# A product and its use placed in different steps, a last layer-1 group of four cut into two, one and one, and a bias as three bf16 terms

## The chip, the cores and the metric

The kernel runs on one core of a Trainium2 chip. The metric is the device time of one execution in microseconds. Three runs of the kernel before gave 1993.61, 1996.18 and 1997.73 us; the median is 1996.18.

The engines are named as in the profile: PE is TensorE (PEld its weight loads), DVE is VectorE, ACT is ScalarE, POOL is GpSimd, and SP is the engine whose queue issues most of the DMAs.

## The reference

Four graph layers run one after the other over 128 graphs of 64 nodes with 128 features. Each adds its result to its input and normalises. Weights, `_layernorm` and `einsum` letters are as usual; everything is float32.

```python
def ssp(x): return softplus(x) - log(2)
# layer 0: d = adj; a filter from 20 Gaussians of d, cut off at 5
f = exp(coeff * (d[..., None] - offsets) ** 2)
W = (ssp(f @ fw1 + fb1) @ fw2 + fb2) * rcut(d)[..., None]
x = layernorm(x + ssp(einsum('bjf,bijf->bif', x @ w_in2f, W) @ ow1 + ob1) @ ow2 + ob2)
# layer 1: the same form with 64 Gaussians and adj as the weight, twice
x = layernorm(x + ...)
# layer 2: three graph convolutions, nA = D^-1/2 (adj + 1) D^-1/2
h = elu(elu(x @ W0 + b0))
h = elu(nA @ (h @ W1) + b1)
x = layernorm(x + nA @ (h @ W2) + b2)
# layer 3: one more, with a small epsilon in the degree
x = layernorm(x + relu((nA3 @ x) @ W3.T + b3))
```

## The kernel before

Two graphs make a *pair* (128 nodes, one per partition), so there are 64 pairs. Only edges that exist are computed: a compaction on DVE (`MAX8`, `FIND_INDEX8`, `MATCH_REPLACE8`, lines 913 to 976) sorts each node's edges into a fixed number of slots. It runs for the first part beside the edge work of the first pairs.

The main loop (line 1504) has 386 iterations. Pairs 0 to 63 are layer 0, 64 to 127 are layer 1, and each pair's edge slots are cut into three chunks, one per iteration. One chunk passes through four stages in three iterations: `filter_in` (PE product `px` on L1410, then two ACT operations that make `h`), `gather` (PE product `pg` on L1436 from a one-hot matrix `hot`, copied by ACT to `g`), `filter_out` (PE product `pw` on L1423) and `message` (DVE `m` on L1451, from `pw` and `g`). After the third chunk eight DVE reductions (L1467, the `sums` queue) add messages into `agg`. PSUM is full: `px` and `pg` have one buffer of two banks each, `pw` has two banks, and a pool `sps_n` with two banks (tag `n`, function `bank`) serves every other product.

When four pairs (a *group*, `GS = 4`) have their sums, the node work of the group follows: `node_after` (products `u`, `o`, `back`, with `na`, `nh`, `no`, `ny` as their uses on ACT and DVE, and a layer norm). In layer 0, `zero_share` (`zT`, `zs`) comes first. After layer 1, `graph_convs` computes layers 2 and 3 of the group: products `gx`, `gh`, `hw`, `nT`, `o`, `sup`, and their uses `gxt`, `em`, `er`, `gy`, `nTs`, `gz`. `node_before` (`xT`, `y`) prepares the features of the group that comes next.

These functions are Python generators. Each `yield` ends a *step*; the loop takes one step from a queue at certain places of an iteration, so that their instructions stand between those of the edges. There are the queues `nodes` (`node_before` and `node_after`) and `convs[0]` and `convs[1]` (graph convolutions of even and odd groups). A step of the kernel before usually holds a product *and* its use:

```python
        y = tiled(f"gy_{name}_{k}")
        nc.vector.tensor_copy(y, ps)      # straight after the four matmuls into ps
```

At the end `in_order` ties every engine's instructions to the order in which the program wrote them, so an engine never takes a later instruction first. Behind the loop a `while` takes steps from the queues in turn until all are empty.

The layer norm takes `bn_stats` and `bn_aggr` per pair on DVE, a power (`rs`, L1175) and one normalisation per pair (L1178) on POOL.

Of the kernel before, what the change touches and what calls it, by code (L numbers as in the profile page):

```python
# [18 lines left out]
P = 128  # L19
A = 64  # L20
# [557 lines left out]
def sparse_stack(ctx: ExitStack, tc: tile.TileContext, t: dict, out: bass.AP, flag):  # L578
# [16 lines left out]
    NG = NP // GS  # L595
# [5 lines left out]
    cpt = ctx.enter_context(tc.tile_pool(name="scompact", bufs=1))  # L601
# [112 lines left out]

    def dram_ap(ap, offset, dims):
        return bass.AP(tensor=ap.tensor, offset=ap.offset + offset, ap=dims)
# [4 lines left out]
    fence, last, kind = None, None, None  # L721

    def act(out_, in_, func, **kw):
        nonlocal fence, last, kind
        now = func == AF.Sin
        if kind is None or now != kind:
            fence = last
            if not now:
                ctx_ = tc.issue_after(fence.ins) if fence is not None else nullcontext()
                with ctx_:  # L730
                    fence = nc.scalar.preload_act_table_set("natural_log_exp_and_others")
            kind = now
        with tc.issue_after(fence.ins) if fence is not None else nullcontext():
            last = nc.scalar.activation(out_, in_, func, **kw)  # L734
        return last
# [24 lines left out]
    ones = const.tile([1, P], F32, name="ones")  # L760
# [76 lines left out]
    def load_row(name, times=1):  # L837
        b = const.tile([1, times * C], F32, name=f"r_{name}")
        nc.scalar.dma_start(b, dram_ap(t[name], 0, [[0, 1], [0, times], [1, C]]))
        return b  # L840
# [206 lines left out]
    def run(queue, n):  # L1047

        while queue and n:
            try:  # L1050
                next(queue[0])
                n -= 1
            except StopIteration:
                queue.popleft()

# [61 lines left out]
    g["b3"] = load_row("L3_gnn_b", GS)  # L1117
# [16 lines left out]
    def late_constants():  # L1134
# [21 lines left out]
        for i in (2, 3):  # L1156
            g[f"blk{i}"] = const.tile([P, GS, P], F32, name=f"blk{i}")
            nc.gpsimd.memset(g[f"blk{i}"], 0.0)
            yield


    def bank(name):
        ps = ps_n.tile([P, 512], F32, tag="n", name=name)
        return ps, ps.rearrange("p (s c) -> p s c", s=GS)

    def layernorm(y, dst, n, name):

        stats = node.tile([P, n, 6], F32, tag=f"st{n}", name=f"st_{name}")
        mv = node.tile([P, n, 2], F32, tag=f"mv{n}", name=f"mv_{name}")
# [3 lines left out]
        rstd = node.tile([P, n], F32, tag=f"rs{n}", name=f"rs_{name}")  # L1173
        nc.vector.tensor_scalar(rstd, mv[:, :, 1], LN_EPS, None, ALU.add)  # L1174
        nc.gpsimd.tensor_tensor(rstd, rstd, neg_half[:, 0:n], ALU.pow)  # L1175
        yield
# [9 lines left out]
    def node_before(layer, q):  # L1186
# [3 lines left out]
        flat, ps = bank(f"xT_{name}")  # L1190
        for s in range(GS):
            nc.tensor.transpose(ps[:, s, :], x_all[:, q * GS + s, :], ident)
        xt = node.tile([P, 512], F32, tag="xt", name=f"xt_{name}")
        nc.vector.tensor_copy(xt, flat)
        yield
        flat, ps = bank(f"y_{name}")
        for s in range(GS):
# [3 lines left out]
        y = node.tile([P, GS, C], F32, tag="y", name=f"ys_{name}", bufs=3)  # L1201
        act(y, ps, AF.Copy)
        feats[layer, q] = y

        xs = x_all[:, q * GS : (q + 1) * GS, :]
        nc.gpsimd.tensor_tensor(xs, xs, w["c2"].unsqueeze(1).to_broadcast([P, GS, C]), ALU.add)
# [5 lines left out]
    def zero_share(q, agg):  # L1212

        rows = node.tile([P, GS, A], F32, tag="zr", name=f"zr_{q}")
        for s in range(GS):
            nc.sync.dma_start(rows[:, s, :], perm[q * GS + s][:, 0:A])
# [5 lines left out]
        flat, ps = bank(f"zT_{q}")  # L1222
        for s in range(GS):
            nc.tensor.transpose(ps[:, s, :], zblk[:, s, :], ident)
        zt = node.tile([P, GS, P], F32, tag="zt", name=f"zt_{q}", bufs=1)
        act(zt, ps, AF.Copy)
        yield
        flat, ps = bank(f"zs_{q}")
        y = feats[0, q]
        for s in range(GS):  # L1230
            nc.tensor.matmul(ps[:, s, :], lhsT=y[:, s, :], rhs=zt[:, s, :], start=True, stop=True)
        nc.vector.scalar_tensor_tensor(agg, ps, zero_filter, agg, ALU.mult, ALU.add)
        yield

    def node_after(layer, q, agg):
# [4 lines left out]
        codes = node.tile([P, GS * P], BF16, tag="cb", name=f"cb_{name}")  # L1240
        nc.sync.dma_start(codes, dram_ap(code_dram[layer], q * GS * P, [[0, P], [1, GS * P]]))
        if layer == 0:
            yield from zero_share(q, agg)
        u, _ = bank(f"u_{name}")
# [3 lines left out]
        a = node.tile([P, 512], F32, tag="na", name=f"na_{name}", bufs=1)  # L1248
        act(a, u, AF.Abs, bias=w["c1"])
        h = node.tile([P, 512], F32, tag="nh", name=f"nh_{name}", bufs=1)  # L1250
        nc.vector.tensor_scalar(h, u, w["c1"], 0.0, ALU.add, ALU.max)
        yield
        act(a, a, AF.Exp, scale=-1.0)

        back = node.tile([P, GS, P], F32, tag="bk", name=f"bk_{name}", bufs=1)
        nc.vector.tensor_scalar(
            back.rearrange("p s i -> p (s i)"), codes, row[:, 0:1], None, ALU.is_equal
        )
        act(a, a, AF.Ln, scale=0.5, bias=half)
# [3 lines left out]
        _, ps = bank(f"o_{name}")  # L1263
        for s in range(GS):
# [3 lines left out]
        o = node.tile([P, GS, C], F32, tag="no", name=f"no_{name}", bufs=1)  # L1268
        act(o, ps, AF.Copy)
        yield  # L1270
        _, ps = bank(f"back_{name}")
        for s in range(GS):
            nc.tensor.matmul(ps[:, s, :], lhsT=back[:, s, :], rhs=o[:, s, :], start=True, stop=True)  # L1273
        y = node.tile([P, GS, C], F32, tag="ny", name=f"ny_{name}", bufs=1)
        xs = x_all[:, q * GS : (q + 1) * GS, :]
        nc.vector.tensor_add(y, ps, xs)
        yield
        yield from layernorm(y, xs, GS, name)
        if layer == 1:
            convs[q % 2].append(graph_convs(q))  # L1280

    def elu(ps, bias, name, twice=False):

        m, r = big(f"em_{name}", 512), big(f"er_{name}", 512)
# [4 lines left out]
        if twice:  # L1289
# [4 lines left out]
        return r  # L1294

    def graph_convs(k):

        pairs = slice(k * GS, (k + 1) * GS)
        xs = x_all[:, pairs, :]

        def tiled(name):
            return big(name, GS * P).rearrange("p (s c) -> p s c", s=GS)

        def scaled(i):

            dinv, blk = g[f"dinv{i}"], g[f"blk{i}"]
            for h in range(2):
# [3 lines left out]
                    dinv[at, pairs].unsqueeze(2).to_broadcast([A, GS, A]), ALU.mult,  # L1311
                )

        def normal(i):

            _, ps = bank(f"nT{i}_{k}")
            for s in range(GS):
                nc.tensor.transpose(ps[:, s, :], g[f"blk{i}"][:, s, :], ident)
            nT = tiled(f"nTs{i}_{k}")
            dinv = g[f"dinv{i}"]  # L1320
            nc.vector.tensor_mul(nT, ps, dinv[:, pairs].unsqueeze(2).to_broadcast([P, GS, P]))
            return nT

        def times(name, lhs, rhs):

            _, ps = bank(f"{name}_{k}")
            for s in range(GS):
                nc.tensor.matmul(ps[:, s, :], lhsT=lhs(s), rhs=rhs(s), start=True, stop=True)  # L1328
            y = tiled(f"gy_{name}_{k}")
            nc.vector.tensor_copy(y, ps)  # L1330
            return y

        scaled(2)
        yield
        nT = normal(2)
        yield
        flat, ps = bank(f"gx_{k}")
        for s in range(GS):
            nc.tensor.transpose(ps[:, s, :], xs[:, s, :], ident)
        xt = big(f"gxt_{k}", 512)  # L1340
        nc.vector.tensor_copy(xt, flat)
        nc.gpsimd.tensor_tensor(xs, xs, g["b2"].unsqueeze(1).to_broadcast([P, GS, C]), ALU.add)
        yield
        flat, _ = bank(f"gh0_{k}")
        nc.tensor.matmul(flat, lhsT=g["W0"], rhs=xt, start=True, stop=True)
# [241 lines left out]
```

## Time and profile before

| | |
|---|---|
| median of three runs | 1996.18 us |
| profiled execution, its own time | 1989.18 us |
| its span, first to last instruction | 1987.4 us |
| granted PE clock over the span | 0.939 |
| busy: PE, DVE, ACT, POOL | 84%, 79%, 72%, 31% |
| HBM traffic | 107 GB/s |
| last chain by engine: PE, DVE, issue, ACT, POOL | 47%, 28%, 9%, 7%, 5% |

The span is the time between the first and the last instruction; the execution's own time has 1.8 us more around it. A busy share is an average over stages that have different limits. A wait row names the waiting instruction, the one that released it, the sum of the waits in us, how many there were, and the longest.

### The profile page before, as it was taken

To read this page: it belongs to the slowest core of one execution; us is meant where nothing else is said; L and a number is where in the kernel's file an instruction comes from. 1 tells how busy PE (TensorE), PEld (TensorE's weight loads), DVE (VectorE), ACT (ScalarE), POOL (GpSimd) and SP (SyncE) were. 2 spreads that over 40 slices of the span, in tenths; PEclk is the share of its full clock that TensorE was granted. 3 is DMA by queue.
4 is the path that set the end of the run, shared out by engine and by line. 5 is a ranking of instruction groups with operands and counts; after the bars stand their busy time and mean duration, and the time that the engine had idled before them with its cause. 6 is when DMAs were issued, how large, how long until landed. Compare 5 with 4: busy or idle time off the path is not lost.

```text
span 1987.4 us, 23539 instructions
## 1 busy us (share of the span) xinstructions
PE 1666.1 (84%) x6796; PEld 806.3 (41%) x6796; DVE 1578.6 (79%) x4249; ACT 1436.7 (72%) x1663; POOL 624.8 (31%) x899
## 2 busy tenths in 40 slices
PE   0298887888788999879989999999999999999874
PEld 0133333343333444334444444444444444444443
DVE  6588878988888777867767888888888887988863
ACT  1277767777677888758888788787787878787720
POOL 2423434432333222251111223233232232323243
PEclk9998888998888999989999999999999999999985
DMA  4354534443444444434656455445454445455300
GB/s 122 83 141 113 129 94 113 112 114 89 113 99 99 116 112 116 105 73 104 142 132 135 103 125 126 109 114 132 111 126 116 114 118 128 115 117 124 72 6 13
DMA packets 120256, 214.95 MB, mean 108 GB/s; under 512 B 41504, under 2 KB 68276, under 8 KB 120116
## 3 DMA queue, kind: packets, MB, share of 16 engines
q1 hardware_dynamic: 111456, 207.19, 44.1%
q0 software_dynamic: 4352, 5.02, 0.8%
q10 hardware_dynamic: 4308, 1.13, 0.3%
q8 instruction: 56, 0.92, 0.2%
q14 instruction: 84, 0.69, 0.1%
HBM read 200.92 MB, written 12.34 MB: 107 GB/s over the span
## 4 chain that ended last, share of the span: by engine, by line
PE 47%; DVE 28%; issue 9%; ACT 7%; POOL 5%; DMA 4%; SPq 0%; DVEq 0%; ACTq 0%; POOLq 0%
PE pw L1423 17%; PE pg L1436 10%; PE px L1410 8%; DVE agg L1467 7%; DVE m L1451 5%; ACT h L734 3%; DVE hot L1395 2%; DVE st L1171 2%; DVE mv L1172 2%; PE back L1273 2%; POOL x_all L1178 1%; PE y L1198 1%; ACT d L734 1%; PE o L1265 1%; PE hw L1328 1%
## 5 line engine op out<-in xcount | busy, mean ns | idle before, releaser
L734 ACT ACTIVATE g<-pg 128x752 f32<-128x752 f32 (+1 forms) x384 | 321.1, 836 | 295.3 <-PE pg L1436 270.1
L1467 DVE TENSOR_REDUCE agg<-m 128x16 f32<-128x336 f32 (+11 forms) x1024 | 417.7, 461 | 1.5
L1423 PE MATMUL pw<-h,w_L_gnn_fw 128*128 128x376 f32 x768 | 321.3, 545 | 107.9 <-DVE m L1451 104.6
L1175 POOL TENSOR_TENSOR rs<-rs,neg_half 128x4 f32<-128x4 f32 x64 | 98.3, 1536 | 951.7 <-DVE rs L1174 860.2
L1423 PE MATMUL pw<-h,w_L_gnn_W2T 128*128 128x432 f32 x768 | 335.4, 561 | 67.1 <-DVE m L1451 67.1
L1436 PE MATMUL pg<-hot,ys 64*128 64x376 f32 (+1 forms) x1536 | 383.9, 578 | 3.2 <-ACT g L734 3.2
L734 ACT ACTIVATE h<-h,half 128x752 f32<-128x752 f32 (+2 forms) x385 | 372.3, 967 | 12.5
L1451 DVE SCALAR_TENSOR_TENSOR m<-pw,c_L_gnn_b,g 128x432 f32<-128x432 f32 x384 | 240.3, 660 | 12.1 <-PE pw L1423 7.7
L1451 DVE SCALAR_TENSOR_TENSOR m<-pw,c_L_gnn_fb,g 128x376 f32<-128x376 f32 x384 | 216.4, 601 | 40.9 <-PE pw L1423 30.0
L1423 PEld LDWEIGHTS pw<-h,w_L_gnn_fw 128*128 128x128 f32 x768 | 143.6, 206 | 229.2 <-DVE m L1451 159.9
L1423 PEld LDWEIGHTS pw<-h,w_L_gnn_W2T 128*128 128x128 f32 x768 | 134.6, 194 | 223.4 <-DVE m L1451 131.1
L734 ACT ACTIVATE h<-px,c_L_gnn_b 128x864 f32<-128x864 f32 x192 | 187.2, 975 | 49.4 <-PE px L1410 49.4
L1436 PEld LDWEIGHTS pg<-hot,ys 64*128 64x128 f32 x1536 | 122.3, 195 | 211.4 <-ACT h L734 104.8
L1395 DVE SCALAR_TENSOR_TENSOR hot<-j,row,w 128x1128 f32<-128x1128 bf16 (+1 forms) x128 | 194.3, 1518 | 0.7
L1410 PE MATMUL px<-d,fw 32*128 32x376 f32 x768 | 178.8, 542 | 2.4 <-ACT d L734 2.4
L1410 PE MATMUL px<-d,w1t 64*128 64x432 f32 x768 | 178.7, 542 | 0.0
L734 ACT ACTIVATE h<-px,c_L_gnn_fb 128x752 f32<-128x752 f32 x192 | 169.4, 882 | 12.1 <-PE px L1410 3.3
L734 ACT ACTIVATE d<-d,neg_off 96x752 f32<-96x752 f32 (+1 forms) x128 | 145.2, 1134 | 0.0
L853 POOL DMA_INDIRECT rows<-comb,goes x64 | 65.2, 1018 | 130.5 <-DMA rows<-comb,goes 98.0
L1410 PEld LDWEIGHTS px<-d,fw 32*128 32x128 f32 x768 | 59.2, 188 | 113.9 <-issue 66.7
L1178 POOL TENSOR_SCALAR x_all<-ny,mv,rs 128x128 f32<-128x128 f32 x128 | 102.9, 813 | 3.3
L1410 PEld LDWEIGHTS px<-d,w1t 64*128 64x128 f32 x768 | 69.0, 187 | 56.8 <-issue 41.8
(208 smaller groups left out, 2029.5 us busy)
## 6 DMA issues: line engine op xcount, KB each, us to landing
d<-d_dram SPq DMA_DIRECT2D x128, 324.0 KB
w<-w_dram SPq DMA_DIRECT2D x128, 324.0 KB
w<-w_dram SPq DMA_DIRECT2D x128, 282.0 KB
j<-j_dram SPq DMA_DIRECT2D x128, 162.0 KB
j<-j_dram SPq DMA_DIRECT2D x128, 141.0 KB
d<-d_dram SPq DMA_DIRECT2D x192, 94.0 KB
x_all<-in_x_dram SPq DMA_DIRECT2D x8, 512.0 KB
cb<-code_dram SPq DMA_DIRECT2D x32, 128.0 KB
```

Of the source, the lines that this page charges most:

```text
L734: last = nc.scalar.activation(out_, in_, func, **kw)
L853: nc.gpsimd.indirect_dma_start(out=into, out_offset=bass.IndirectOffsetOnAxis(ap=at, axis=0), in_=rows, in_offset=None,)
L1171: nc.vector.bn_stats(stats[:, s, :], y[:, s, :])
L1172: nc.vector.bn_aggr(mv[:, s, :], stats[:, s, :])
L1175: nc.gpsimd.tensor_tensor(rstd, rstd, neg_half[:, 0:n], ALU.pow)
L1178: nc.gpsimd.tensor_scalar(dst[:, s, :], y[:, s, :], mv[:, s, 0:1], rstd[:, s : s + 1], ALU.subtract, ALU.mult,)
L1395: nc.vector.scalar_tensor_tensor(hots[n][:, 0:size], j[:, 0:size], near, wt[:, 0:size], ALU.is_equal, ALU.mult)
L1410: nc.tensor.matmul(ps[:, b, 0:n], lhsT=w["w1"][rows, :], rhs=d[rows, col : col + n], start=True, stop=True,)
L1423: nc.tensor.matmul(ps[:, 0 : c["size"]], lhsT=c["w"]["w2"], rhs=c["h"][:, b, :], start=True, stop=True)
L1436: nc.tensor.matmul(ps[:, b, 0:n], lhsT=y[rows, :], rhs=hots[c["n"]][rows, at], start=True, stop=True,)
L1451: nc.vector.scalar_tensor_tensor(messages[n][:, b, at], c["pw"][b][:, 0:size], c["w"]["b2"], c["g"][:, b, :], ALU.add, ALU.mult,)
L1467: nc.vector.tensor_reduce(av[:, :, :, r], v[:, :, :, BASES[layer][r] : BASES[layer][r] + CAPS[layer][r]], AX.X, ALU.add,)
```

## The change

- A step that ends in a PE product now yields `True`, and its use on DVE or ACT stands in the next step. A function `slot` takes one step of a queue; if it ended in a product, that queue is *owing*, and the next `slot` of a queue that is not empty first takes its own step and then the owed one.
- `node_before` has a queue of its own (`befores`). The order inside an iteration changes: sums, compaction, side work and the one-hot come first; then `filter_in`, the slots of nodes and befores; then `filter_out`, `message`, the first convs slot, Gaussians, `gather`, and the second convs slot (a second nodes slot when there are no convs).
- `GROUPS`: layer 1 has fifteen groups of four, then one of two pairs and two of one. Those three do not enter `nodes` and `convs`; each has a lane in `last`, gets two slots in an iteration, and goes from `node_after` straight into `graph_convs`.
- The pool of the compaction is closed at iteration 195, and a pool `srings` takes its place: four buffers per lane for the convs, and a block matrix `blocks` per lane in place of `blk2` and `blk3`.
- The last bias, a float32 row added by a float32 product with `ones` (L1368), is split once into three bf16 terms whose sum is the row; the product then has three rows in bf16.
- In the layer norm the power moves from the step of the statistics to the step of the normalisations; in `node_before` the addition of `c2` moves ahead of the product `y`; in `graph_convs` the normalised matrix for layer 2 is made after `hw1` instead of at the start, and the scaling for layer 3 right after `o2`. `zero_share` waits one step more after its loads.

The core of the diff:

```diff
+    GROUPS = [[slice(GS * q, GS * (q + 1)) for q in range(NP // GS)]] * 2
+    GROUPS[1] = GROUPS[1][:-1] + [slice(NP - 4, NP - 2), slice(NP - 2, NP - 1), slice(NP - 1, NP)]
...
+    def load_terms(name):
+        b = const.tile([1, C], F32, name=f"r_{name}")
+        nc.scalar.dma_start(b, t[name].rearrange("(o p) -> o p", o=1))
+        part_ = const.tile([1, 3, C], BF16, name=f"p_{name}")
+        for i in range(3):
+            nc.vector.tensor_copy(part_[:, i, :], b)
+            if i < 2:
+                nc.vector.tensor_sub(b, b, part_[:, i, :])
+        terms = const.tile([3, GS, C], BF16, name=f"t_{name}")
+        for s in range(GS):
+            nc.scalar.dma_start(terms[:, s, :], part_[0:1].rearrange("o i c -> o (i c)"))
+        return terms
...
         rstd = ...
         nc.vector.tensor_scalar(rstd, mv[:, :, 1], LN_EPS, None, ALU.add)
+        yield
         nc.gpsimd.tensor_tensor(rstd, rstd, neg_half[:, 0:n], ALU.pow)
-        yield
...
         nc.tensor.matmul(
             u, lhsT=w["o1"], rhs=agg.rearrange("f s r -> f (s r)"), start=True, stop=True
         )
+        yield True
         a = once("na", n, q)
         act(a, u, AF.Abs, bias=w["c1"])
+        act(a, a, AF.Exp, scale=-1.0)
         h = once("nh", n, q)
         nc.vector.tensor_scalar(h, u, w["c1"], 0.0, ALU.add, ALU.max)
         yield
-        act(a, a, AF.Exp, scale=-1.0)
...
         if layer == 1:
-            convs[q % 2].append(graph_convs(q))
+            if n < GS:
+                yield from graph_convs(q)
+            else:
+                convs[q % 2].append(graph_convs(q))
...
+    def slot(queue):
+        nonlocal owing
+        if not queue:
+            return
+        before, owing = owing, None
+        held = run(queue, 1)
+        if before is not None and before is not queue:
+            run(before, 1)
+        if held:
+            owing = queue
...
     for i in range(3 * N + 2):
+        run(sums, 3)
+        run(early, 7)
+        run(side, 1)
...
-            filter_in(c)
-        run(nodes, 1)
-        if c is not None and k == 0:
-            one_hot(n)
-        run(sums, 3)
-        run(early, 7)
-        run(side, 1)
+                one_hot(n)
+            filter_in(c)
+        slot(nodes)
+        if k < 2:
+            slot(befores)
+        for queue in last:
+            slot(queue)
         if c2 is not None:
             filter_out(c2)
             message(c2)
+        slot(convs[0])
         if k < 2 and n + 1 < N:
             gaussians(n + 1, k)
-        run(convs[0] or nodes, k == 2 or bool(convs[0]))
         if c1 is not None:
             gather(c1)
-        run(convs[1], 1)
+        slot(convs[1] if convs[0] or convs[1] else nodes)
+        for queue in last:
+            slot(queue)
```

## The prediction

> **What bounds the kernel now.** I read the page's busy shares first, then the busy time by stage, then the waits inside each stage, and last the end of the chain. The shares alone do not name a bound:
>
> ```profile
> span 1987.4 us, 23539 instructions
> ...
> PE 1666.1 (84%) x6796; PEld 806.3 (41%) x6796; DVE 1578.6 (79%) x4249; ACT 1436.7 (72%) x1663; POOL 624.8 (31%) x899
> ```
>
> The stages do. Columns: window, its length, then busy us (instructions) of PE, weight loads, DVE, ACT and POOL, then clock, DMA share, GB/s. The windows are layer 0 while edges are still compacted, the rest of layer 0, layer 1, and the tail after the last edge product.
>
> ```profile
> 100.00:620.00 520.00, 431.44 (x1636) 193.66 (x1635) 443.64 (x1687) 378.45 (x462) 185.11 (x340) 0.90 0.45 110
> 620.00:1030.00 410.00, 364.72 (x1512) 168.69 (x1510) 309.09 (x659) 334.70 (x408) 111.79 (x142) 0.95 0.46 112
> 1030.00:1900.00 870.00, 805.55 (x3422) 400.45 (x3421) 724.17 (x1519) 697.76 (x763) 259.07 (x290) 0.98 0.50 115
> 1904.00:1988.00 84.00, 44.53 (x166) 31.78 (x164) 38.93 (x109) 6.60 (x10) 35.20 (x43) 0.63 0.04 11
> ```
>
> In layer 1 PE is busy 93% and idle 64 us. In the first window it is idle 89 us, in the second 45. The waits of layer 1 say for what (us in total, times, longest):
>
> ```profile
> PE pw L1423 <- DVE m L1451: 63.9, 39, 3.2
> DVE nh L1251 <- ACT na L734: 51.4, 15, 4.6
> ...
> DVE ny L1276 <- PE back L1273: 15.6, 15, 2.1
> DVE gz L1374 <- PE o L1370: 12.7, 7, 1.9
> ...
> DVE em L1285 <- PE gh L1351: 8.3, 7, 1.3
> ```
>
> All of PE's idle time in layer 1 is the edge product `pw` waiting for the message `m` that frees its bank, and `m` is late because DVE stood still ahead of it, waiting for a node or conv product issued just before. DVE's waits of this kind (the rows shown, and `em` on L1345, `gz` L1359, `gy`, `xt`, `gxt`, `nTs`) add to 126 us; with 724 busy that is 850 of 870, so DVE and PE bound together. In the first window the same sum is nh 18.1 + zblk 11.2 + ny 8.6 + agg 4.8 + xt 0.3 = 43 us beside 444 busy of 520; PE waits 67.5 for `m`. In the second it is nh 21.7 + ny 17.5 + agg 14.1 + zblk 3.7 = 57 us; PE waits 40.4, of which one wait of 12.1 belongs to the `dinv` power on POOL, which stays.
>
> The tail lasts from the last `pw` (ends 1904.6) to 1987.4: 83 us in which no engine is busy 55%. It is one chain of four-pair operations, at a low clock: the `hw` product of four pairs takes 1.05 us at 1330 and 2.04 at 1957.7.
>
> **What the Trainium skill says.** "PSUM — Partial Sum Buffer", section Engine vs sequencer instructions: the queues of ScalarE, VectorE and GpSimdE are strict FIFO. The trace agrees: DVE idles up to 4.6 us at `nh` with ready messages behind it. The same page, section PSUM bank collisions raise a hardware error, says two engines must not read one bank at once; that is why `nh` waits for ACT's `na` although both read only `u` (at 1330 `na` ends at 1330.42 and `nh` starts at 1330.45). So this wait is not removed by a later place, only overtaken. "TensorE: Matmul & The Clock Gate", section Back-to-back issue gap, gives 518 cycles at 2.4 GHz for N=512 in bf16, 0.22 us; no bf16 product is in this trace.
>
> **The change part by part.** The sum is made against the profiled execution, 1989.18 us (the span and 1.8 around it); it lies 7.0 under the median 1996.18, and I carry the difference over to the median.
>
> *Steps that part product and use.* No steady instruction goes away. In the changed order of instructions the use of a product from the first slot stands behind the two messages (2 x 0.62 us) instead of ahead of sums and messages, and that of the convs' first slot behind the gather (0.83 us of PE). Of `nh`'s 3.0 us per wait, 1.2 is overtaken by the messages alone and more by the three reductions now ahead. What can be won is the smaller of DVE's product waits and PE's waits for `m`: 43 in the first window, 40.4 - 12.1 = 28 in the second, 64 in the third; together **135**. I take half, **-68**, for two reasons: ACT is busy 80% in layer 1 and `px` and `pg` have one buffer each, so it becomes late next; and 30 of 334 DVE uses now stand behind three reductions and a one-hot (1.2 + 1.5 us), holding their bank that long. Ends: 0 and -135; below nothing is the rival with the banks.
>
> *Order inside the iteration.* Sums, compaction, side work and one-hot move ahead of the node step on DVE; messages keep the same work before them. On SP the six or seven loads of a pair come behind the compaction's stores (some 0.6 us each); the first of them is used three iterations (14 us) later, which hides it; without that cover 8 parts x 2 layers x 3 stores x 0.6 = +29. The extra empty step between the `zr` loads and `zblk` costs nothing, since the nodes queue has two slots per iteration there; it may save some of the 11.2 us above. On POOL `pow` moves one step back to its normalisations and the `c2` addition one forward; POOL is busy 30% there: 0, at most +3.
>
> *Bias.* L1368 has 32 passes at some 0.5 us from start to start, 16 us; 18 bf16 products at the page's 0.22 are 4. PE is the bound of only part of layer 1, so of 12 I take **-6**; ends 0 and -12. The terms add five DVE operations on one partition (each under 0.3 us by the 128x64 rows) and four small loads on ACT's queue at the start; DVE stands idle from 39.6 to 53.6 for the `ad` landing and ACT until 79.8, so at most **+1**.
>
> *Pools and lanes.* Per-lane blocks replace two shared ones: five memsets on an idle POOL, 0 to +2. Closing the compaction pool makes the first memset wait for stores that ended long before.
>
> *The tail.* Groups of four end at pair 59; then come two, one and one, with two more `cb` loads and two more stores on SP, each as early as its lane. Before, group 14's convs and all of group 15 are left when the edges end. After, the order leaves the end of 13's convs, nearly all of 14's, and the lanes of two, one and one, taken in turn. From that order, with a 128x512 DVE operation at 0.69 us and a 128x128 one at about 0.25 (estimated from 0.69 less 384 elements at the same rate), DVE has 37 us left. POOL has 13 powers x 1.03, 28 normalisations x 0.78, and blocks and bias additions of some 7: 42 us. So POOL is the floor. The last pair's own chain is short: 11 products at 0.5, 15 DVE operations at 0.35, three layer norms at 0.65 on DVE and 1.8 on POOL, 7 ACT at 0.3 and 35 handovers at 0.05: some 22 us, with the store 25. Five lanes through in-order queues do not reach the floor; between 45 and 72 I take 58: **-25**.
>
> Sum: -68 - 6 - 25 + 1 = **-98**: own time 1891, on the level of the median **1898**.
>
> **The rivals.** (a) *ACT takes the bound.* For: ACT is busy 3.76 us per iteration in edges alone and DVE 4.2 of 5.0, so three engines are within 15% of each other. Against: ACT waits 116 us for `pg` in layer 1, so it has room. Steady gain a fifth, 14, with tail 22: 1960. (b) *All of it comes.* The clock of 0.90 in the first window rises too, since PE idles less; 135 + 12 + 30: 1819. (c) *The banks decide, and it is slower.* The pool `sps_n` has two banks for four queues. Before, the use was issued straight behind its product; now two products are open at once, and the third waits for a use issued only one slot earlier. Price: 30 uses behind the one-hot x 2.7 = 81, and the other 350 products at 0.3 each (messages and use, 1.24 + 0.69, less gather and `px` of 1.66 that PE does meanwhile) = 105; 186 against the 98: +88, 2084. It decides once a product waits on average over 98/382 = 0.26 us. Against it: PE has 2.6 us of own work between a conv product and the third one. (d) *The parts do not separate in layer 0,* where only the nodes queue has work: then the gain is layer 1's half and the tail, 32 + 6 + 25: 1933. The order of instructions speaks against it: `nh` stands behind the messages there too.
>
> **How the numbers follow.** Forecast 0.52; (a) 0.17; (b) 0.13; (d) 0.06; (c) 0.10; no change 0.02. A measurement of this kernel tells about 0.2%, 4 us, from nothing. Faster: all but (c) and no change, less a little of (a): 0.87; same 0.03; slower 0.10. The range leaves out (c) and most of (b): 1838 to 1964. The likeliest is 1898.
>
> **What would show it.** Right: in layer 1 `pw <- m` below 40 us, `nh <- na` below 20, `ny`, `gz`, `em`, `gy` nearly gone from DVE's waits, an iteration of 4.7 us instead of 5.0 (132 `h<-px` between 1230 and 1890); in the first window 4.5 instead of 4.8 (108 in 520); 55 to 60 us after the last `pw`, POOL busiest. Wrong: node and conv products (`o`, `hw`, `gh`, `nT`) waiting on PE for DVE or ACT uses, which is (c); ACT over 90% with `px <- h`, which is (a); a tail over 70 us.

## The result: slower by 1.5%

The changed kernel takes 2025.4 us (median of four runs, 2021.7 to 2027.3) where the kernel before takes 1995.0 in the same session: a ratio of 1.0148, 95% interval 1.0129 to 1.0168. Forecast were 1898 us and a range of 1838 to 1964. The profiled execution took 2027.3, its span 2025.5.

The busy shares of the changed kernel's page say as little as those of before: PE 83%, DVE 78%, ACT 71%, POOL 31%.

To compare stages, I cut both executions at the same work, not at the same time: at the start of `hot` of pairs 8, 52, 72, 120 and 124 (pairs 0 to 63 are layer 0). The busy time in such windows of the changed kernel (columns as in the prediction; pairs 8 to 52, 52 to 72, 72 to 120, and 124 to the end):

```profile
208.20:857.40 649.20, 539.17 (x2046) 245.95 (x2042) 506.03 (x1666) 457.09 (x568) 208.29 (x383) 0.90 0.40 101
857.40:1137.30 279.90, 236.21 (x917) 106.04 (x918) 198.09 (x408) 209.29 (x247) 63.40 (x55) 0.93 0.45 106
1137.30:1837.80 700.50, 646.93 (x2833) 325.50 (x2830) 597.48 (x1262) 572.16 (x627) 218.76 (x246) 1.00 0.51 121
1897.70:2025.50 127.80, 95.06 (x404) 56.60 (x402) 93.75 (x251) 54.64 (x74) 55.34 (x77) 0.83 0.14 35
```

The kernel before needs 610.6, 262.3, 710.8 and 146.5 us for the same; its first and third windows are

```profile
198.40:809.00 610.60, 521.55 (x2048) 237.85 (x2046) 502.89 (x1671) 461.59 (x568) 209.88 (x384) 0.91 0.45 108
...
1071.30:1782.10 710.80, 660.60 (x2832) 330.19 (x2831) 595.96 (x1251) 570.63 (x625) 215.65 (x242) 0.98 0.51 119
```

So layer 0 lost 39 + 18 us (and 7 more in pairs 0 to 8), layer 1 gained 10, and the end gained 19. The waits of pairs 8 to 52 show what layer 0 lost:

```profile
ACT h L740 <- PE px L1457: 107.6, 47, 8.5
...
DVE zblk L1254 <- DMA zr<-perm: 40.4, 11, 6.1
...
PE zT L1258 <- DVE zblk L1254: 38.0, 11, 6.6
...
PE o L1302 <- DVE nh L1298: 22.9, 11, 2.6
PE y L1232 <- DVE xt L1226: 21.8, 11, 3.5
...
PE pw L1470 <- DVE m L1498: 9.7, 13, 1.5
```

In the kernel before, the same stretch had

```profile
PE pw L1423 <- DVE m L1451: 70.0, 41, 4.6
...
DVE zblk L1220 <- DMA zr<-perm: 13.0, 6, 5.1
```

The wait that I wanted gone is gone: `pw` behind `m` was 70.0 us and is 9.7. In its place PE stands eleven times, once in each group, at `zT`, at `o` and at `y`; `px`, queued behind them, comes late, and ACT waits 107.6 us for it. `y` waits for `xt`, the separated use of the product before. `o` waits for the addition that ends `nh`, two steps behind the uses of `u`. At `zT` the cause is a transfer: `zblk` on DVE waits for the `zr` loads, 40.4 us instead of 13.0, and `zT` waits for `zblk`.

Layer 1, pairs 72 to 120:

```profile
DVE m L1498 <- PE pw L1470: 73.7, 54, 3.2
...
ACT h L740 <- PE px L1457: 61.1, 53, 2.3
...
PE o L1402 <- DVE gy_hw L1374: 15.7, 11, 2.1
PE u L1282 <- DVE agg L1516: 11.3, 11, 1.3
...
PE pw L1470 <- DVE m L1498: 2.5, 3, 1.3
```

DVE's waits for node and conv products (`ny`, `gz`, `em`, `gy`) nearly vanished, and PE's wait for `m` fell from 49.8 to 2.5 us. But window length less busy time gives PE 50.2 us idle before and 53.6 now, DVE 114.8 and 103.0. The waits changed names far more than they shrank. The 10 us that the stage gained are not idle time: PE's busy time fell from 660.6 to 646.9 us.

The timeline around one group shows the stall. First SP's queue in the changed kernel (start, duration, instruction):

```profile
474.35 0.45 SPq L1037 DMA_DIRECT2D j<-j_dram  x1
...
476.12 0.59 SPq L1037 DMA_DIRECT2D w<-w_dram  x1
476.76 0.58 SPq L1278 DMA_DIRECT2D cb<-code_dram  x1
477.39 1.85 SPq L1249 DMA_DIRECT2D zr<-perm  x4
```

and DVE in the same microseconds:

```profile
472.94 1.38 DVE L1442 SCALAR_TENSOR_TENSOR hot<-j,row,w 128x1128 f32<-128x1128 bf16 x1
...
482.26 0.59 DVE L1254 TENSOR_SCALAR zblk<-zr 64x256 f32<-64x256 f32 x2 [1.74 <-DMA zr<-perm]
```

`j` and `w` of the pair after next go into the buffers that `hot` reads, so they start when `hot` ends, at 474.3. `zr` needs nothing of `hot`, but stands behind them and is issued at 477.39. DVE reaches `zblk` 7.6 us after the start of `hot` (at 480.52) and then stands until 482.26. The same group in the kernel before, first from SP's queue, then from DVE:

```profile
451.88 1.85 SPq L1216 DMA_DIRECT2D zr<-perm  x4
...
445.69 2.06 DVE L1395 SCALAR_TENSOR_TENSOR hot<-j,row,w 128x1128 f32<-128x1128 bf16 x1
...
456.82 0.59 DVE L1220 TENSOR_SCALAR zblk<-zr 64x256 f32<-64x256 f32 x2 [0.24 <-DMA zr<-perm]
```

There too `zr` follows `hot`, and `zblk` starts 4.9 us after the first `zr` issue, as it does now. But DVE reached `zblk` 10.9 us after `hot` and found the loads all but landed. In the timeline of DVE three messages and three rounds of sums and compaction stood between the two, and in the new order it is two of each. Over the eleven groups of pairs 8 to 52 the median of that way is 10.3 us before and 7.2 now. "PSUM — Partial Sum Buffer", section Engine vs sequencer instructions, of the Trainium skill speaks of strict order for the queues of ScalarE, VectorE and GpSimdE; here SP's DMA queue shows the same.

### The profile page after: what moved, and what is told of

Read it like the earlier page. It is cut to its first block, busy times and chain, and to the rows that moved or that the text cites. A ratio compares the mean times of both kernels' runs of the same rounds, so it can differ in the third digit from the quotient of the medians.

```text
span 2025.5 us, 23645 instructions
## 1 busy us (share of the span) xinstructions
PE 1675.1 (83%) x6790; PEld 808.6 (40%) x6790; DVE 1589.7 (78%) x4298; ACT 1433.8 (71%) x1679; POOL 632.0 (31%) x920
## 4 chain that ended last, share of the span: by engine, by line
PE 36%; DVE 34%; DMA 8%; issue 6%; ACT 6%; SPq 5%; POOL 3%; DVEq 0%; POOLq 0%; ACTq 0%
PE pw L1470 11%; DVE m L1498 8%; PE px L1457 7%; DVE agg L1516 7%; PE pg L1483 6%; DVE hot L1442 5%; ACT h L740 3%; DMA zr<-perm 3%; SPq L1037 3%; DVE st L1200 2%; DVE mv L1201 2%; DMA w<-w_dram 2%; PE y L1232 2%; PE back L1311 1%; PE u L1282 1%
## 5 line engine op out<-in xcount | busy, mean ns | idle before, releaser
L1483 PE MATMUL pg<-hot,ys 64*128 64x376 f32 (+1 forms) x1536 | 379.0, 571 | 3.0 <-DVE hot L1442 2.7
L740 ACT ACTIVATE h<-h,half 128x752 f32<-128x752 f32 (+2 forms) x385 | 372.3, 967 | 12.6
L1205 POOL TENSOR_TENSOR rs<-rs,neg_half 128x4 f32<-128x4 f32 (+2 forms) x70 | 69.9, 998 | 946.1 <-DVE rs L1203 920.8
L1470 PE MATMUL pw<-h,w_L_gnn_fw 128*128 128x376 f32 x768 | 330.8, 558 | 26.3 <-DVE m L1498 23.9
L1498 DVE SCALAR_TENSOR_TENSOR m<-pw,c_L_gnn_b,g 128x432 f32<-128x432 f32 x384 | 245.6, 663 | 117.3 <-PE pw L1470 95.5
L1470 PE MATMUL pw<-h,w_L_gnn_W2T 128*128 128x432 f32 x768 | 325.1, 546 | 4.2 <-DVE m L1498 4.2
L1457 PE MATMUL px<-d,fw 32*128 32x376 f32 x768 | 188.2, 568 | 21.2 <-ACT h L740 18.3
L1442 DVE SCALAR_TENSOR_TENSOR hot<-j,row,w 128x1128 f32<-128x1128 bf16 (+1 forms) x128 | 188.4, 1472 | 0.0
L1457 PE MATMUL px<-d,w1t 64*128 64x432 f32 x768 | 182.8, 553 | 0.0
L1207 POOL TENSOR_SCALAR x_all<-ny,mv,rs 128x128 f32<-128x128 f32 x128 | 118.5, 936 | 3.6
L1457 PEld LDWEIGHTS px<-d,fw 32*128 32x128 f32 x768 | 61.8, 196 | 107.2 <-issue 46.7
```

Of the source, the lines that this page charges most:

```text
L740: latest = nc.scalar.activation(out_, in_, func, **kw)
L1207: nc.gpsimd.tensor_scalar(dst[:, s, :], y[:, s, :], mv[:, s, 0:1], rstd[:, s : s + 1], ALU.subtract, ALU.mult,)
L1442: nc.vector.scalar_tensor_tensor(hots[n][:, 0:size], j[:, 0:size], near, wt[:, 0:size], ALU.is_equal, ALU.mult)
L1457: nc.tensor.matmul(ps[:, b, 0:n], lhsT=w["w1"][rows, :], rhs=d[rows, col : col + n], start=True, stop=True,)
L1470: nc.tensor.matmul(ps[:, 0 : c["size"]], lhsT=c["w"]["w2"], rhs=c["h"][:, b, :], start=True, stop=True)
L1483: nc.tensor.matmul(ps[:, b, 0:n], lhsT=y[rows, :], rhs=hots[c["n"]][rows, at], start=True, stop=True,)
```

## The experiments

All timed kernels ran beside runs of the kernel before on the same chip, whose median lay between 1987 and 2001 us. Each ratio is to that kernel before. Two kernels timed at different times can therefore differ by some us for no reason of their own; where the ratios give another size than the medians, it is given too. This table gives the stages of each profiled execution, cut at the `hot` of the pairs named; the start of the program, which the stages leave out, differs by up to 9 us between these executions.

| kernel | median us | pairs 0-8 | 8-52 | 52-72 | 72-120 | 120-124 | 124-end |
|---|---|---|---|---|---|---|---|
| before | 1995.0 | 104.8 | 610.6 | 262.3 | 710.9 | 58.8 | 146.5 |
| changed | 2025.4 | 111.8 | 649.2 | 279.9 | 700.5 | 59.9 | 127.8 |
| zr_early | 1905.9 | 100.8 | 564.0 | 255.5 | 699.6 | 59.9 | 129.3 |
| zr_steps | 1945.6 | 103.1 | 593.5 | 264.6 | 700.0 | 59.9 | 126.9 |
| zr_pool | 1974.0 | 107.2 | 618.1 | 267.2 | 700.2 | 59.8 | 134.6 |
| zr_mixed | 1871.0 | 99.0 | 563.4 | 255.1 | 670.0 | 56.8 | 132.8 |
| mixed_joined | 1929.3 | 109.7 | 600.1 | 265.5 | 668.7 | 56.7 | 130.8 |
| joined | 1998.2 | 113.5 | 640.9 | 271.9 | 686.4 | 56.0 | 133.3 |
| old_order | 1976.9 | 109.4 | 638.8 | 283.7 | 670.1 | 55.8 | 133.7 |
| joined_old_order | 1909.2 | 108.5 | 587.5 | 255.1 | 667.6 | 55.7 | 136.0 |
| old_steps | 1963.0 | 111.3 | 587.7 | 256.5 | 711.5 | 59.0 | 147.1 |
| nT_first | 1955.4 | 111.1 | 593.1 | 258.2 | 701.9 | 57.3 | 145.0 |

**The zr loads earlier (zr_early).**

```diff
 # slot_sums, where a group's first sums begin (s == 0)
+            if layer == 0:
+                zeros[q] = node.tile([P, GS, A], F32, tag="zr", name=f"zr_{q}")
+                for i in range(GS):
+                    nc.sync.dma_start(zeros[q][:, i, :], perm[q * GS + i][:, 0:A])
...
 # zero_share
...
-        for s in range(n):
-            nc.sync.dma_start(rows[:, s, :], perm[first + s][:, 0:A])
-        yield
-        yield
+        n, rows = agg.shape[1], zeros.pop(q)
```

> Edit: the changed kernel, but the four zr loads of a layer-0 group are issued when the group's first sums are (three pairs earlier), and the two steps between them and zblk are gone. Theory Z (the zr loads stand on SP's queue behind j and w loads that wait for a late hot, and zblk then holds DVE): the 59 us of `zblk <- zr` and the 51 us of `zT <- zblk` go, about -40 us, 1985. Theory S (the next product stands on PE and waits for the separated use): those waits stay and PE meets them elsewhere, -10 at most, 2015 to 2025. Theory O (one_hot behind sums and compaction makes hot and with it the gathering late, whatever zr does): -10 at most, 2015 to 2025.

1905.9 us, ratio 0.9551 (0.9511 to 0.9592): 119 us less than the changed kernel, three times what theory Z gave. The window of pairs 8 to 52:

```profile
196.70:760.60 563.90, 500.19 (x2044) 228.24 (x2041) 499.27 (x1666) 455.21 (x566) 203.60 (x383) 0.97 0.46 117
```

and its PE waits:

```profile
PE pw L1465 <- DVE m L1493: 21.1, 25, 2.2
...
PE o L1297 <- DVE nh L1293: 9.2, 11, 1.6
```

`zblk <- zr` and `zT <- zblk` are gone, but so is `y <- xt`, and `o <- nh` has more than halved. And PE's own busy time for the same products fell from 539 to 500 us while the granted clock rose from 0.90 to 0.97. Of the 85 us gained in this stretch PE idled 46 less and was busy 39 less. So more than the wait went away: this edit also takes out two steps, and the next two runs part the two.

**The queue and the steps (zr_pool, zr_steps).** One issues the loads at the changed place on POOL's queue (`nc.gpsimd.dma_start`); the other has early loads and keeps the two `yield`s.

> Edit: the changed kernel, but the four zr loads of a group are issued on POOL's queue in place of SP's, at the same step and with the same two steps to zblk. Theory Q (what holds zr is the queue: it stands behind j and w loads that wait for hot): the `zblk <- zr` wait falls from 59 us to under 20 and the time comes near the early loads' 1906: 1905 to 1935. Theory D (two steps are too short a distance whatever the queue): the wait stays above 40 us and the time within 20 of 2025. POOL issues 64 more DMAs; its own work is off the path, so at most +10 from that.

> Edit: early zr loads as before, but the two empty steps ahead of zblk stay, so that every later step of the node chain stands where the changed kernel has it. Theory W (what the early loads gained is the wait of zblk and PE for zr alone): 1906 again, within 8. Theory P (the two steps also shift the node chain so that its products fall next to node_before's and wait for uses, as with the zr loads on POOL's queue, where zblk waits 15 us in pairs 8 to 52 and PE still 22 us for nh and 21 us for xt): 1955 to 1985, with `o <- nh` and `y <- xt` near 20 us each in that stretch.

zr_pool: 1974.0 us, 0.9933 (0.9912 to 0.9955). The wait for `zr` falls over the whole span from 59.0 to 19.7 us, as theory Q said, but the time only by 51 (43 by the ratios); Q's range was missed, and D's too. So the queue is what makes the loads late: `hot` and `zblk` stand where they stood. zr_steps: 1945.6 us, 0.9766 (0.9733 to 0.9799). PE's waits in its pairs 8 to 52:

```profile
PE y L1232 <- DVE xt L1226: 22.7, 11, 3.5
...
PE o L1299 <- DVE nh L1295: 20.5, 11, 2.6
```

With no wait for `zr` left, the two steps alone bring these back, as theory P said, but they cost 40 us and not 49 to 79. So the 119 us part into 80 for the late `zr` loads and 40 for the place of the node chain (76 and 43 by the ratios): two steps further on, in layer 0 one iteration, `o` and `y` meet PE before DVE has done their operands. One of the two steps stood in the kernel before as well; what it cost there was not tried.

**Product and use rejoined, and the old order (joined, old_order, joined_old_order).**

```diff
 # joined: in slot()
         held = run(queue, 1)
+        if held:
+            held = run(queue, 1)
 # old_order: in the loop
-        run(sums, 3)
-        run(early, 7)
-        run(side, 1)
...
-                one_hot(n)
             filter_in(c)
         slot(nodes)
+        if c is not None and k == 0:
+            one_hot(n)
+        run(sums, 3)
+        run(early, 7)
+        run(side, 1)
```

> Edit: the changed kernel, but a step that issues a product is followed at once by the step with its use; order inside the iteration, tail and bias stay as changed. Theory S: the layer-0 loss comes back, about -50, 1975, and layer 1 is slower by some us at most. Theory Z: fewer steps, but the zr loads stand where they stood: within 12 of 2025. Theory O: the same, 2025.

> Edit: the changed kernel with the old order inside the iteration: filter_in, node step, one_hot, and only then sums, compaction and side steps; separation, tail and bias stay. Theory O: hot is early again, -50, 1975. Theory Z: hot early, so the j and w loads ahead of zr are released early; the `zblk <- zr` wait falls to about 15 us as before, -40, 1985. Theory S: products still wait for their uses, within 10 of 2025.

> Edit: both, so that of the change only the shorter tail, the bias terms and the queue of its own for node_before are left. If separation and order are the whole cause of the loss: before less about 19 for the tail and 7 for the bias, about 1969. If it stands at 1990 or more, the loss sits in something else (the separate queue of node_before, the smaller pools). Theory S alone: equal to the joined kernel. Theory O alone: equal to the old-order kernel.

1998.2 us, 1.0033 (1.0015 to 1.0051); 1976.9 us, 0.9909 (0.9876 to 0.9942); and 1909.2 us, 0.9571 (0.9531 to 0.9610). No single theory fits all three. `zblk` waits for `zr` in pairs 8 to 52 by 41.5 us in the joined kernel and by 7.0 and 7.3 in those with the old order, and the median way from `hot` to `zblk` is 7.1, 10.3 and 10.3 us. All three keep the two steps between the loads and `zblk`, so the stall belongs to the order, neither to the separation nor to the extra step by itself. The three, with the changed kernel, also give the size of each part: the new order costs 89 us without the separation and 48 with it. The separation costs 27 us in the new order (23 by the ratios) and 68 in the old one. There PE waits, in pairs 8 to 52, 36.1 us for `nh` and 35.1 for `xt` (0.3 and 1.1 without the separation); that it is the three reductions, which then stand between a product and its use, is argued from the order and was not tried alone. A joined kernel takes a product and its use in one slot, so its chains also run ahead by a step each time; the distance between the two and the phase of the chain are not told apart by these runs. In pairs 72 to 120 the joined kernel, without the separation, already has `pw <- m` at 2.9 us (14.4 with the old order), and the separation on top of it costs 14 us there. What I did not foresee is the third kernel: without separation it beats the kernel before by 82 us, 43 of them in pairs 72 to 120.

**The order by layer, and the separation on top of it (zr_mixed, mixed_joined).** Early loads; sums and one-hot first where `n < NP or n >= N - GS`, behind the node step elsewhere. mixed_joined adds the two lines of `joined`.

> Edit: early zr loads, and the place of sums and one_hot by layer: ahead of the products in layer 0 and in the last four pairs as changed, behind the first node step as of old in layer 1's other pairs; products and uses stay separate. If order and zr add up stage by stage (layer 0 from hot of pair 8 to pair 52 563.9 us with early zr, layer 1 from pair 72 to pair 120 670.1 us with the old order against 699.6): 1906 - 30 = 1876, within 8. If the gain of the old order in layer 1 was only late layer-0 work caught up: 1900 or more.

> Edit: the kernel with early zr loads and the order by layer (1871), but a product's step is followed at once by its use. If the separation is worth something where zr is out of the way: slower by 15 to 30 (layer 0 of the joined kernel with the old order took 587.5 us from pair 8 to 52 against 563.9), 1886 to 1900. If all that the separated kernels gained came from the order, the early loads and the queues: 1871 or less.

zr_mixed: 1871.0 us, 0.9419 (0.9379 to 0.9460), 5 under the sum of the stages; it is the fastest of all, 116 us under the kernel before in the same session. mixed_joined: 1929.3 us, 0.9681 (0.9649 to 0.9713). So the separation is worth 58 us (52 by the ratios) once `zr` is out of its way, nearly twice the upper end of what I expected. Pairs 8 to 52 of zr_mixed:

```profile
190.20:753.70 563.50, 503.29 (x2044) 228.90 (x2041) 498.85 (x1668) 455.28 (x566) 203.22 (x383) 0.96 0.48 117
```

and of mixed_joined:

```profile
205.20:805.40 600.20, 519.41 (x2038) 240.71 (x2034) 502.90 (x1667) 461.68 (x566) 208.72 (x381) 0.92 0.45 110
```

All of it is layer 0: 11 + 37 + 10 us by the first three stages of the table. In pairs 72 to 120 the two differ by 1.3 us, the joined one ahead. Nor is it the wait that the separation was made for: `pw <- m` is 20.4 us in both in pairs 8 to 52. What differs most is another wait, in zr_mixed and then in mixed_joined:

```profile
PE o L1297 <- DVE nh L1293: 9.0, 11, 1.6
...
PE o L1297 <- DVE nh L1293: 31.8, 11, 3.9
```

PE idles 20.6 us less in zr_mixed and is busy 16 us less, at a clock of 0.96 instead of 0.92. `nh` here is no separated use but the end of the node chain, so the steps that the separation adds seem to move `o` to where its operand is ready. With the two steps ahead of `zblk` it is the other way: 22.9 us in the changed kernel, 10.8 in the joined one. That other places for the steps would do the same without a separation was not tried.

**Which move costs layer 1 its 30 us (sums_late, hot_late).** From zr_early, with only the sums, or only the one-hot, put back behind the node step in layer 1.

> Edit: the kernel with early zr loads; in layer 1 (but its last four pairs) the sums go behind the first node step as of old, and one_hot stays ahead of filter_in. If the sums ahead of the node step cost the 35 us (they hold DVE for three reductions before it serves the use that the next product and px wait for): about 1871, as with both moved back. If one_hot ahead does (1.38 us on DVE before the node step's use, once in three iterations): 1900 or more.

> Edit: the kernel with early zr loads; in layer 1 (but its last four pairs) one_hot goes behind the first node step as of old, and the sums stay ahead. The counterpart: 1900 or more if the sums cost the 35 us, about 1871 if one_hot does; between, if both share it.

1879.5 us, 0.9417 (0.9363 to 0.9472), and 1888.6 us, 0.9454 (0.9398 to 0.9509). Pairs 72 to 120 take 672.5 and 687.3 us, against 699.6 with neither and 670.0 with both. The sums carry 27 of the 30 us; with the sums still ahead, a late one-hot gives back 12. The two overlap. DVE's wait for `pw` in that stretch, 71.4 us in zr_early, goes with the sums. hot_late:

```profile
DVE m L1493 <- PE pw L1465: 65.2, 52, 2.5
```

sums_late:

```profile
DVE m L1493 <- PE pw L1465: 23.0, 35, 1.8
```

That fits the reason named ahead of the run, three reductions ahead of the use for which `px` waits; the trace does not show that chain link by link.

**Where layer 1 gained without separation (one_queue, one_ring, old_steps, exp_late, power_early, nT_first).** All on joined_old_order. one_queue appends `node_before` to `nodes` again; one_ring gives both lanes one ring of eight buffers; exp_late, power_early and nT_first put back one part each of the old steps in the chains, old_steps all three. With the old place of `nT` come a buffer of its own for it and three ring buffers instead of four for the small groups. The core of nT_first:

```diff
         scaled(2)
+        yield
+        nT = yield from normal(2)
+        yield
         flat, ps = bank(f"gx_{q}", n)
...
-        nT = yield from normal(2)
-        yield
         flat, ps = bank(f"gh1_{q}", n)
...
-        scaled(3)
         yield True
         z = by_pair(tiled("gz2", n, q))
         nc.vector.tensor_add(z, ps, xs)
         yield
+        scaled(3)
```

> Edit: on the joined kernel with the old order (1909), node_before goes back into the queue of node_after, and the second place of the iteration serves that queue only at k = 2, as in the kernel before. The joined kernel with the old order is 82 us faster than before, of which the bias is about 12 and the split about 11. If the queue of its own is the rest: 1960 to 1970. If not: 1905 to 1915.

> Edit: on the joined kernel with the old order (1909), the convolutions of both lanes share one ring of eight buffers, as in the kernel before, in place of four for each lane. If a lane that waits for the other's buffers cost the kernel before much in layer 1 (710.8 us from pair 72 to 120 against 667.6): slower by 20 to 30, 1930 to 1940. If not: 1905 to 1915.

> Edit: on the joined kernel with the old order (1909), the steps inside the chains as before: nT of the second convolution ahead of gx, scaled(3) behind gz2, POOL's power in the step of the statistics, Exp a step later; nT gets a buffer of its own, the small groups' rings three in place of four. If this order of steps kept DVE waiting for PE in the convolutions (xt, gy, em, gz: about 50 us of DVE's waits in layer 1 before, 15 in the joined kernel with the old order): slower by 20 to 33, 1930 to 1942. If not: 1904 to 1916.

> Edit: on the joined kernel with the old order (1909), only Exp of the node chain goes a step later, to Ln. If the wait of nh for na is the lever (49.7 us in layer 1 with all old steps, 29.9 without): layer 1 from pair 72 to 120 690 to 711 us, 1930 to 1955. If not: 667 to 672, 1905 to 1915.

> Edit: on the same kernel, only POOL's power goes back to the step of the statistics. If POOL, standing at a power that waits for DVE's variance, made the normalisations and the c2 and b2 additions behind it late and PE's products with them: 680 to 711 us in that stretch, 1925 to 1955. If POOL has room (32% busy): 667 to 672, 1905 to 1915.

> Edit: on the same kernel, only the convolution's steps as before: nT of the second convolution ahead of gx with a buffer of its own, scaled(3) behind gz2. If the convolutions' place against the node chain is the lever (gz, nTs, gxt waits, and pw behind m 49.6 against 14.4 us): 690 to 711 us in that stretch, 1930 to 1955. If not: 667 to 672.

one_queue: 1935.0 us, 0.9700 (0.9629 to 0.9770); the queue of its own is worth 26 us, all in layer 0 (pairs 72 to 120 take 664.0), not the 55 that I looked for; one_queue's four runs spread from 1917 to 1942 us, so this size is rough. one_ring: 1912.0, 0.9583 (0.9549 to 0.9617); exp_late: 1916.6, 0.9590 (0.9516 to 0.9664); power_early: 1910.9, 0.9561 (0.9485 to 0.9638). None of the three moves pairs 72 to 120 by more than 3.1 us. old_steps: 1963.0, 0.9829 (0.9765 to 0.9893), with 711.5 us in pairs 72 to 120, as before the change. nT_first: 1955.4, 0.9784 (0.9710 to 0.9858). It carries 34 of these 44 us. The waits of pairs 72 to 120, joined_old_order:

```profile
DVE nh L1290 <- ACT na L740: 29.9, 12, 4.5
...
PE pw L1470 <- DVE m L1498: 14.4, 19, 2.3
DVE ny L1315 <- PE back L1311: 13.5, 12, 1.5
```

nT_first:

```profile
PE pw L1471 <- DVE m L1499: 52.4, 35, 3.2
DVE nh L1290 <- ACT na L740: 49.8, 12, 5.5
...
DVE ny L1315 <- PE back L1311: 22.8, 11, 2.1
...
DVE gz L1422 <- PE o L1419: 12.8, 10, 1.7
```

So the wait for `m` that I set out to explain in the kernel before comes back with the place of `nT` and `scaled(3)` and the buffers that go with it. That place shifts every later convolution step against the node chain; which of the two moves does it, and which meeting of the chains makes `nh` and `m` late, was not tried.

**The tail and the bias undone (even_tail, f32_bias).** On the changed kernel: `GROUPS[1]` left at sixteen groups of four; the bias again one f32 row and a product of f32 ones.

> Edit: the changed kernel with layer 1 in sixteen groups of four (the line that splits the last group taken out). The trace of the changed kernel is 18.7 us shorter from hot of pair 124 to the end than that of before, so the split's theory: +19 from the whole part, 2044; rival: the separation and the order gave part of these 18.7 us, since the joined kernels with the split have 133 to 136 us there against 127.8 and 146.5: then +11 to +13, 2037.

> Edit: the changed kernel with the last bias as one f32 row and a product of f32 ones. If PE sets the pace in layer 1: sixteen products of four f32 passes in place of one bf16 pass, +6 to +10, 2033. If PE waits there anyway for uses (DVE's m waits for pw 73.7 us in that stage), most of it is hidden: 0 to +4, 2027.

2030.8 us, 1.0224 (1.0179 to 1.0268), and 2031.7 us, 1.0240 (1.0189 to 1.0291). The medians put the split at 5 us and the bias at 6, the ratios at 15 and 18: the kernel before was 8 us faster beside these two than beside the changed kernel, so neither size is sharp. The stages of the profiled executions lie between. In even_tail the part from pair 124 to the end takes 138.4 us against 127.8: 10.6 from the split. In f32_bias pairs 72 to 120 take 710.3 and the end 130.6: 9.8 and 2.8 from the bias. So the split gave only a part of the 18.7 us, as its rival said. The bias gave at least what the first of its two theories said, and its 9.8 us are nearly all that pairs 72 to 120 gained over the kernel before.

## Why the prediction was wrong

- **What failed, in the sum.** The order inside the iteration was put at 0 and the separation at -68, the rest at -30. joined_old_order has only the rest of the change and is 82 us faster than the kernel before; order and separation together add 116 us to it (2025.4 against 1909.2). So the sign is wrong because of these two terms, and the rest hid much of it.
- **Order inside the iteration: 0, at most +29.** This is the step that failed first: it costs 48 us with the separation and 89 without. "The extra empty step between the `zr` loads and `zblk` costs nothing" counted slots, not what SP has in front of `zr`. The `j` and `w` loads of a pair wait for `hot`, the `zr` loads stand behind them, and DVE reached `zblk` some 3 us sooner after `hot` than before (7.6 against 10.9 in the two groups shown). The late loads measured 80 us, the shift of the node chain by the two steps 40. I bounded the cost of late pair loads and never asked what waits behind them, although 11.2 of the 43 us that I counted as waits to be won in the first window were `zblk` waiting for `zr`. Moving the sums and the one-hot ahead cost 30 us more in pairs 72 to 120.
- **Parting product and use: -68, from 43, 28 and 64 halved.** The sum let a later use win DVE's waits and gave PE no wait for that use; only rival (c) had one. In the changed kernel the separation costs 27 us: PE stands at `y` for 21.8 us in pairs 8 to 52 where the joined kernel has 0.8. With the early loads and the order by layer its size, 52 to 58 us, is near the forecast, but that is luck: it came in layer 0, where the prediction had half of 71, with `pw <- m` unchanged, and nothing came in layer 1, where it had half of 64.
- **The 64 us of layer 1.** PE's wait for `m` was real, and came down to 2.5 us. The reason given for it was incomplete: in pairs 72 to 120, without the separation, a later `nT` and an earlier `scaled(3)` bring the wait from 52.4 to 14.4 us, edits that I did not cost at all, and the new order brings it on to 2.9. Nor did I cost the queue of its own for `node_before`, worth 26 us.
- **Bias: -6**, ends 0 and -12. By the two stages it is -12.6, all of the 12 that I halved; by the times between -6 and -18. The products of L1368 took 19.8 us of PE, those of L1413 now take 6.7. The 0.22 us for one that the prediction took from a page is lower than this trace: behind the one at 1199.50 the next product starts 0.31 us later, which makes some 5.6 us (an estimate, 18 times 0.31) where the sum had 4.
- **Tail: -25.** From pair 124 to the end it is -18.7, of which the split gave 10.6. From the end of the last `pw` (1961.9) to the end it is 63.6 us against the 58 forecast; even_tail has 77.2 there. POOL was not the busiest engine there: DVE was busy 38.2 us, PE 35.6, POOL 34.4.
- **Rivals.** Of (c) the sign came, and its sign for the trace, products that wait on PE for uses. But its mechanism did not: by the wait rows they wait for their operands, not for a bank, and zr_mixed with the same two banks and the same separation takes 1871 us. (a) did not come: ACT is busy 82% in pairs 72 to 120 and waits 119 us for `px` and `pg`. (b) and (d) are ruled out by the loss in layer 0.
- **What would show it.** `pw <- m` below 40, `nh <- na` below 20, `ny`, `gz`, `em`, `gy` gone in layer 1: all came, and did not mean what I took them for. The iteration did not: 700.5 us over 144 iterations of pairs 72 to 120 are 4.86 us, not 4.7, and 649.2 over 132 of pairs 8 to 52 are 4.92, not the 4.5 forecast for the first window. zr_mixed has 4.65 and 4.27.

## What to carry to other kernels

When a step with a load moves, look at what stands ahead of it on the load's own queue and what those instructions wait for; a small load behind two that wait for a buffer is as late as they are. A wait that disappears from the list is no gain until the idle time of the engine that sets the pace falls too: here PE's wait for messages fell by 47 us in a stage and its idle time rose by 3. Parting a product from its use is worth what the order around it makes of it: on this one kernel some -55, +27 or +68 us. My reading, which no run tests by itself, is that it pays when the work between them on the user's engine is shorter than the way to the next product.

## What was not expected of the hardware

- **Waits cost PE twice.** For the same products in pairs 8 to 52 PE was busy 539 us at a granted clock of 0.90 in the changed kernel and 500 us at 0.97 with early loads. One wait shows how. PE stands 2.52 us for `zblk` ahead of `zT` at 482.90, the group shown above; then the clock is halved for 6.8 us, and `px`, `pw` and `pg` take 1.58, 2.88 and 1.63 us, where they took 0.90, 1.53 and 0.90 just before. The two windows, columns as above:

```profile
480.20:483.60 3.40, 0.88 (x8) 0.53 (x6) 1.59 (x6) 1.02 (x2) 0.00 (x0) 1.00 0.55 133
483.60:490.40 6.80, 6.80 (x17) 3.07 (x18) 6.21 (x16) 4.00 (x6) 3.33 (x16) 0.50 0.06 21
```

"TensorE: Matmul & The Clock Gate", section Part 1: The HAM clock gate (the "warmup" mystery), of the Trainium skill says that an idle window of about 3.4 us throttles the PE to half its clock. Here the wait was shorter, and PE was busy 0.88 us of the window ahead of the half clock; so by this trace the window need not be wholly idle. That the waits at `zT` alone lowered the mean clock is not shown: zr_pool, with `zT <- zblk` down to 13.3 us, still has 0.91, as the kernel before has.

- **A few steps of phase weigh as much as a mechanism.** Two empty steps in the node chain cost 40 us of 1946, and the place of one transposed matrix and one scaling in the convolutions 34 us in one stage, with the same products and uses in both.
